# The first loads dealt to two hardware queues, and gate's first weights loaded in halves, in a planned mixture-of-experts kernel

## The chip, the core and the metric

The kernel runs on one core of one Trainium2 chip. The metric is the device time of one execution, in microseconds (us). A profiled execution adds a trace of every engine: PE (TensorE, the matrix engine), ACT (ScalarE), DVE (VectorE), POOL (GpSimd) and SP (SyncE, which here only issues transfers).

## The reference

Nine feed-forward blocks (eight experts and a shared one) are applied to 16 blocks of 256 tokens by 256 features, and their results are mixed with factors of each batch row:

```
g = einsum('bsd,edf->ebsf', h, Wg)          # e = 8, d = 256, f = 1024, float32
u = einsum('bsd,edf->ebsf', h, Wu)
expert_outs = einsum('ebsf,efd->ebsd', silu(g) * u, Wd)
expert_output = einsum('be,ebsd->bsd', gating_probs, expert_outs)
shared = (silu(h @ Sg) * (h @ Su)) @ Sd
x = x + (1 - sg) * expert_output + sg * shared
```

## The kernel before

The work is cut into 72 units: nine sets of weights, two halves of the 1024 hidden features, four groups of four token blocks. Products of several token blocks are not made one by one: the kernel forms sums and differences of inputs and of weights ahead (fast matrix multiplication in the manner of Winograd and Strassen), so TensorE does fewer products and VectorE, GpSimd and ScalarE do more additions. Unit 0 is different. Its weights' sums are not ready yet, so its products are made plainly, one block at a time. These are the "single-block products" of the title, in `unit_up_w` under `if n == 0`.

Nothing is scheduled by hand. Every operation is handed to `Plan.add` with an engine, an assumed length and a rank. `Plan.run` then plays the program through with these lengths: on each engine it takes, of the operations whose inputs are ready and whose buffers are free, the one of the lowest rank. PE alone keeps two strictly ranked lines, one for the products into the `dn` banks and one for all else. The order that comes out is written down engine by engine, and each engine executes its own list strictly in order. So a rank or an assumed length changes the lists, and the lists alone reach the chip. The dictionary `RANK` (lines 25 to 33) holds the constants of these ranks.

What happens at the start matters here. Nine products of zeros (L354) keep PE at work while the first data comes. `make_raw` loads two blocks of x (tile `side`, 256 KB each), transposes each on PE (L561, into `dn`) and copies it with ACT into `pq` (L566). `load_base` loads the upper 128 rows of gate's weights into the first part of a `wb` tile (256 KB) and `load_raw` the lower 128 rows into another `wb` tile (256 KB); up's weights come in the same way. In unit 0 the product of one chunk of 128 hidden features with one token block takes two accumulating matmuls, one with each weights tile. The first two chunks of the first pair of blocks are done one block at a time (moving operand 256 wide, tile X), all later ones for two blocks at once (512 wide, X for gate and M for up).

All these loads go through one helper, whose `engine` argument was left at SP for every load:

```
def load(rank, dst, src, kb, deps=(), new=(), uses=(), late=0, engine="SP"):
    queue = {"SP": nc.sync, "ACT": nc.scalar}[engine]
```

SP's list therefore begins: x block 0, gate's upper rows, gate's lower rows, x block 1, up's upper rows, up's lower rows, x blocks 2 and 3, then gate's and up's other row blocks for the sums, and eight more blocks of x (tiles `h`). PE's list begins, behind the zeros: transposes of block 0; two X products of chunk 0 and one of chunk 1 with block 0; transposes of block 1; the other five X products; two M products; transposes of blocks 2 and 3. A float32 matmul stands in the trace as two records. Two small loads, `p_bc` and `coef` (the mixing factors, spread over all 128 partitions), go out from POOL's queue at the start, and the sums on `wb` and `wp` (L366) begin on POOL once the later weights have landed.

From unit 4 to unit 55 the kernel is in its long middle phase with sums kept in DRAM (tiles `star`); from unit 56 on it uses the other form again and finishes the output.

Of the kernel before, what the change touches and what calls it, by code (L numbers as in the profile page):

```python
# [16 lines left out]
P = 128  # L17
# [5 lines left out]


RANK = {
    "first": 4, "q": 2.85, "dc": 2.45, "acc": 2.55, "g": -5.35, "cp": 1.85, "seed": -0.3, "s": 0.75,
    "lagx": 1.0, "sc": 15.85, "bank": (6.6, 7.1, 8.6, 15.9, 16.4, 16.9, 17.3), "ev": 0.3, "p": 2.3,
    "xc": 0.2, "st": 1.2, "qa": -2.0, "da": -1.25, "ga": -7.25, "pace": 2, "m0": 1.9, "m1": 2.5, "xm":
    0, "w": 16, "mp": 4, "m2": 1.5, "ml": 1.75, "lagw": 1.0, "wp": -0.95, "wq": -0.9, "wqa": -2.25,
    "wdc": 2.2, "ws": 0.5, "wseed": 0.2, "wxc": 0.95, "pa": -4.25, "hd": (), "ph": 7.25, "pd": 1.0,  # L30
    "xh": 5, "hX": 4.5, "hA": 10.5, "hR": 5.0, "hD": -6.5, "hE": 5, "hF": -7.75, "hG": -3.75, "to":
    (-18, -3, -9, -16, -46), "back": (-27, 120, 21, -15, -5, 80, 20),
}


# [169 lines left out]
def kernel(  # L205
# [177 lines left out]
    def load_base(m, e, half, rank, ranks=None):  # L383
        b = Buf("wb", f"wb_{m}_{e}_{half}")
        src = [
            sources(e)[m][ts(part, P), ts(half, 4 * P)].rearrange("p (c q) -> p c q", q=P)
            for part in range(2)
        ] if m < 2 else None
        late = 0 if rank < 0 else 8
        ru, rv = ranks or (rank, rank)  # L390
        if m == 2:
            rows = sources(e)[2][ts(half, 4 * P), :].rearrange("(c p) (k q) -> p c k q", p=P, q=P)
        if m == 2:
            u = v = load(ru, lambda: b.tile, rows, 512, [], [b], late=late)
        else:
            u = load(ru, lambda: b[:, :, 0, :], src[0], 256, [], [b], late=late)
            v = load(rv, lambda: b[:, :, 1, :], src[1], 256, [], [], [b], late=late)
        ops = []
        for i, t in enumerate(POINTS):
            r, x_ = (lambda i=i: b[:, i, 1, :]), (lambda i=i: b[:, i, 0, :])  # L400
            if t == 0:
                op = v
            elif abs(t) == 1:
                op = tt("POOL", rank + 1, r, r, x_, ALU.add if t > 0 else ALU.subtract, P, [u, v], uses=[b])
            elif e == half == 0:
                op = stt(rank + 1, r, x_, float(t), r, ALU.add, P, [u, v], uses=[b])
            else:
                twice = Buf("wp", f"twice_{m}_{e}_{half}")
                op = add(
                    "ACT", act(P), rank + 1, lambda: nc.scalar.mul(twice[:, 0, :], x_(), float(t)), [u, v], [twice], [b]  # L410
                )
                op = tt("POOL", rank + 1, r, r, lambda: twice[:, 0, :], ALU.add, P, [op], [], [b, twice])
            ops.append(op)
        base[m, e, half], baseop[m, e, half] = b, (u, ops)

    def make_pair(m, e, half, k, rank):
        i, j = PAIRS[k]
        d = POINTS[j] - POINTS[i]
        w, (u, rops) = base[m, e, half], baseop[m, e, half]
        b = Buf("wp", f"wp_{m}_{e}_{half}_{k}")  # L420
        r = tt(
            "POOL", rank, lambda: b[:, 0, :], lambda: w[:, j, 1, :], lambda: w[:, i, 1, :], ALU.subtract, P,
            [rops[i], rops[j]], [b], [w],
        )

        def rr():
            return b[:, 0:1, :].broadcast_to([P, 2, P])

        def uu():
            return w[:, i : j + 1 : j - i, 0, :]  # L430

        if d == 1:
            o = tt("POOL", rank, lambda: b[:, 1:3, :], rr, uu, ALU.subtract, 2 * P, [r, u], [], [b, w])
        elif e == 0 and half == 1 and m in RANK["hd"]:
            o = stt(rank, lambda: b[:, 1:3, :], uu, -float(d), rr, ALU.add, 2 * P, [r, u], [], [b, w])
        else:
            o = add(
                "ACT", act(2 * P), rank - RANK["pa"], lambda: nc.scalar.mul(b[:, 1:3, :], uu(), float(d)), [r, u], uses=[b, w]  # L438
            )
            o = tt("POOL", rank, lambda: b[:, 1:3, :], rr, lambda: b[:, 1:3, :], ALU.subtract, 2 * P, [o], [], [b])  # L440
        pair[m, e, half, k], pairop[m, e, half, k] = b, o

    def load_raw(ranks):

        b = Buf("wb", "wb_raw")
        ops = [
            load(
                ranks[m], lambda m=m: b[:, :, m, :],
                sources(0)[m][ts(1, P), 0 : 4 * P].rearrange("p (c q) -> p c q", q=P), 256,
                [], [b] if m == 0 else [], [b] if m else [],  # L450
            )
            for m in range(2)
        ]
        return b, ops

    def load_down(e, half, rank):
# [196 lines left out]
    def diagonal(n, m, unit, a, rank, pq, consume):  # L653

        e, half, g = unit
        w, (u, rops) = base[m, e, half], baseop[m, e, half]
        xb, xo = xd[g, a], xdop[g, a]
        name = f"{m}_{n}_{a}"
        bank = Buf("D", f"D_{name}")
# [3 lines left out]
        for h, i in enumerate((2 * a + 1, 2 * a)):  # L663
            ps.append(
                mm(
                    MM, rank + 1 / 8 + h / 100, lambda h=h: bank[:, h, :], lambda i=i: w[:, i, 0, :],
                    lambda i=i: xb[:, i % 2, :], h == 0, True, h == 1, [u, xo[i][0], *ps],
                    [bank] if h == 0 else [], [w, xb] if h == 0 else [w, xb, bank],
                )
            )  # L670
# [14 lines left out]
        ops = {}  # L685
# [86 lines left out]
    def unit_up_w(n, unit):  # L772
# [41 lines left out]
        if n == 0:  # L814
            w, wops = first_raw
            readers = {0: [], 1: []}
            for step, (a, c) in enumerate((a, c) for a in range(2) for c in range(4)):
                xb, xo = raw[a]
                for m in range(2):
                    b0, (u, _) = base[m, e, half], baseop[m, e, half]  # L820
                    bank = Buf("XM"[m], f"plain_{m}_{a}_{c}")
                    r = 2.6 * step - 7 + m / 2

                    def view(k, xb=xb):
                        return xb.tile[:, 2 * k : 2 * k + 2, :]

                    if m == 0 and step < 2:

                        m1 = None
                        for h in range(2):  # L830
                            rh = -7 + h / 5 + step / 20
                            for k, (wv, wo) in enumerate(
                                ((lambda b0=b0, c=c: b0[:, c, 0, :], u), (lambda c=c: w[:, c, 0, :], wops[0]))
                            ):
                                m1 = mm(
                                    MM, rh + k / 100, lambda bank=bank, h=h: bank[:, h, :], wv,
                                    lambda xb=xb, k=k, h=h: xb.tile[:, 2 * k + h, :], h == k == 0, k == 1, h == 1,
                                    [wo, xo[h], m1], [bank] if h == k == 0 else [],
                                    [w if k else b0, xb] if h == k == 0 else [w if k else b0, xb, bank],
                                )  # L840
                        readers[a].append(m1)
                        gate(f"p{step}")(bank, [m1], r + 0.6, [(c, 2 * a), (c, 2 * a + 1)])
                        continue
                    m0 = mm(
                        2 * MM, r, lambda bank=bank: bank[:, :, :], lambda b0=b0, c=c: b0[:, c, 0, :],
                        lambda view=view: view(0), True, False, False, [u, *xo], [bank], [b0, xb],
                    )
                    m1 = mm(
                        2 * MM, r + 0.1, lambda bank=bank: bank[:, :, :], lambda m=m, c=c: w[:, c, m, :],
                        lambda view=view: view(1), False, True, False, [m0, wops[m], *xo], [], [w, xb, bank],  # L850
                    )
                    readers[a].append(m1)
                    (gate, mult)[m](f"p{step}")(bank, [m1], r + 0.6, [(c, 2 * a), (c, 2 * a + 1)])
# [231 lines left out]
    def unit_down(n, unit, hb, pairs, acc, state):  # L1085
# [3 lines left out]
        for k, (i, j) in enumerate(PAIRS):  # L1089
# [4 lines left out]
            work.append((lambda w=w: w[:, 0, :], wo, lambda gb=gb: gb[:, :], [go], [w, gb]))  # L1094
            work.append((lambda w=w: w[:, 1, :], wo, lambda hbuf=hbuf: hbuf[:, 1, :], lo, [w, hbuf]))
            work.append((lambda w=w: w[:, 2, :], wo, lambda hbuf=hbuf: hbuf[:, 0, :], lo, [w, hbuf]))
        w, (u, rops) = base[2, e, half], baseop[2, e, half]
        for at in range(8):
            i, part = (3 - at, 0) if at < 4 else (at - 4, 1)
            work.append(  # L1100
                (lambda i=i, part=part: w[:, i, part, :], rops[i] if part else u, lambda at=at: acc[:, at, :],
                 state["acc"], [w, acc])
            )
        ev, evops = None, []
# [258 lines left out]
    for n, unit in enumerate(units):  # L1363
# [51 lines left out]
            unit_down(n, unit, *unit_up(n, unit))  # L1415
            continue
        for k in range(NG):
            if n == LAST + min(11 + k, int(RANK["m0"] + RANK["m1"] * k + RANK["m2"])):
                merge(k, W * (LAST + RANK["m0"] + RANK["m1"] * k))
        hb, hops = unit_up_w(n, unit)  # L1420
        if n == end:
# [83 lines left out]
```

## Time and profile before

| | |
|---|---|
| median of 3 runs | 2485.02 us (2485.01 to 2485.07) |
| the profiled execution | 2482.88 us |
| its span, first to last instruction | 2480.8 us |
| PE busy in the span | 2469.3 us |
| DVE, POOL, ACT busy | 1857.2, 1807.2, 1606.0 us |
| bytes moved by DMA | 525.08 MB, mean 212 GB/s |

The span is what the trace shows; the execution's own time is 2.1 us longer, and the unprofiled median lies another 2.1 us higher. PE works through nearly the whole span, so the time can only be shortened where PE stands still or where it would do less.

### The profile page before, as it was taken

How to read it: one execution, taken by the hardware profiler on the slowest of the kernel's cores; microseconds unless marked ns; L12 is line 12 of the kernel's file. 1: busy time of each engine (PE TensorE's matmuls, PEld its weight loads, DVE VectorE, ACT ScalarE, POOL GpSimd, SP SyncE). 2: the span in 40 equal slices, each digit the busy share in tenths (PEclk: the TensorE clock that was granted, in tenths of full speed). 3: DMA queues.
4: the chain of work that ended last, by engine and by line, in shares of the span. 5: the costliest groups of instructions: out<-in, count | busy, mean ns of one | idle time of the engine just before them, and what ended most of it. 6: DMA issues, size and time to landing. Idle time of an engine off the chain costs nothing.

```text
span 2480.8 us, 35084 instructions
## 1 busy us (share of the span) xinstructions
PE 2469.3 (100%) x10894; PEld 2055.7 (83%) x10894; DVE 1857.2 (75%) x3142; ACT 1606.0 (65%) x3373; POOL 1807.2 (73%) x1947
## 2 busy tenths in 40 slices
PE   9999999999999999999999999999999999999999
PEld 5778888888888888888888888888888777777777
DVE  6787777777777777777767777777777788888787
ACT  3357777777787777777777777777777333333331
POOL 6886777768585868677776858586766687877874
PEclk9999999999999999999999999999999999999999
DMA  7545688888898888898888898888888877887666
GB/s 254 184 159 213 211 218 222 209 216 211 222 218 220 207 206 216 213 221 215 216 204 223 210 223 213 208 211 207 220 213 226 235 202 202 217 223 208 172 191 208
DMA packets 195769, 525.08 MB, mean 212 GB/s; under 512 B 16864, under 2 KB 83440, under 8 KB 186112
## 3 DMA queue, kind: packets, MB, share of 16 engines
q0 software_dynamic: 39552, 214.52, 45.1%
q1 hardware_dynamic: 156032, 308.33, 36.2%
q8 instruction: 87, 1.43, 0.2%
q14 instruction: 98, 0.80, 0.1%
HBM read 290.53 MB, written 232.26 MB: 211 GB/s over the span
## 4 chain that ended last, share of the span: by engine, by line
PE 99%; ACT 1%; DMA 0%; DVE 0%; issue 0%; SPq 0%; DVEq 0%
PE dn L647 33%; PE X L647 25%; PE M L647 20%; PE D L647 20%; DMA wb<-in_L_cond_Wg_dram 0%; PE dn L1311 0%; ACT sg L894 0%; PE dn L522 0%; ACT sg L885 0%; PE dn L561 0%; ACT wp L438 0%; SPq L361 0%; DVE X L366 0%; DVEq L1500 0%; ACT pq L674 0%
## 5 line engine op out<-in xcount | busy, mean ns | idle before, releaser
L366 POOL TENSOR_TENSOR s<-pq,pq 128x512 f32<-128x512 f32 x852 | 1116.0, 1337 | 450.0 <-DVE X L366 347.1
L366 DVE TENSOR_TENSOR X<-M,s 128x512 f32<-128x512 f32 x697 | 466.8, 692 | 155.7 <-PE M L647 98.9
L647 PE MATMUL X<-xp,wp 128*128 128x256 f32 x2204 | 570.2, 379 | 0.0
L647 PEld LDWEIGHTS X<-xp,wp 128*128 128x128 f32 x2204 | 418.4, 190 | 82.8 <-issue 24.6
L647 PE MATMUL D<-xd,wb 128*128 128x256 f32 x1760 | 454.6, 380 | 1.4 <-ACT sg L894 0.8
L647 PE MATMUL M<-xp,wp 128*128 128x256 f32 x1732 | 448.3, 379 | 0.3 <-DVE X L366 0.3
L647 PEld LDWEIGHTS D<-xd,wb 128*128 128x128 f32 x1760 | 333.2, 190 | 74.5 <-issue 22.9
L885 ACT ACTIVATE sg<-sg,coef 128x256 f32<-128x256 f32 x832 | 393.1, 510 | 2.4
L647 PEld LDWEIGHTS M<-xp,wp 128*128 128x128 f32 x1732 | 328.8, 190 | 70.6 <-issue 23.2
L1123 ACT COPY ev<-dn 128x512 f32<-128x512 f32 x451 | 261.7, 587 | 137.7 <-PE dn L647 134.7
L366 DVE TENSOR_TENSOR pq<-D,pq 128x256 f32<-128x256 f32 x568 | 229.9, 416 | 107.6 <-PE D L647 101.0
L921 DVE TENSOR_TENSOR big<-big,X 128x1024 f32<-128x1024 f32 x233 | 281.6, 1209 | 0.0
L647 PE MATMUL dn<-h,wp 128*128 128x256 f32 x1040 | 271.6, 379 | 0.5 <-ACT ev L1123 0.4
L366 DVE TENSOR_TENSOR X<-X,sg 128x512 f32<-128x512 f32 x233 | 162.0, 695 | 110.9 <-ACT sg L885 68.9
L674 ACT COPY pq<-D 128x512 f32<-128x512 f32 x284 | 167.2, 589 | 114.4 <-PE D L647 108.0
L647 PEld LDWEIGHTS dn<-h,wp 128*128 128x128 f32 x1040 | 197.2, 190 | 29.4 <-POOL wp L366 0.8
L894 ACT ACTIVATE sg<-X 128x512 f32<-128x512 f32 x236 | 142.0, 602 | 109.0 <-PE X L647 107.4
L647 PE MATMUL dn<-h,low 128*128 128x512 f32 (+1 forms) x498 | 199.0, 503 | 0.0
L1046 ACT COPY ev<-dn 128x512 f32<-128x512 f32 x123 | 72.0, 586 | 163.9 <-PE dn L647 162.7
L1123 ACT COPY big<-dn 128x512 f32<-128x512 f32 x225 | 130.8, 587 | 69.2 <-PE dn L647 67.3
L366 DVE TENSOR_TENSOR low<-X,h 128x256 f32<-128x256 f32 x233 | 97.5, 419 | 94.2 <-ACT h L969 93.8
L647 PE MATMUL M<-xp,low 128*128 128x256 f32 x592 | 157.5, 379 | 0.0
(161 smaller groups left out, 3911.2 us busy)
## 6 DMA issues: line engine op xcount, KB each, us to landing
xp<-keep_p SPq DMA_DIRECT2D x408, 384.0 KB, 5.0
star<-ev POOLq DMA_DIRECT2D x105, 768.0 KB, 6.9
xd<-keep_d SPq DMA_DIRECT2D x136, 512.0 KB, 3.6
star<-big POOLq DMA_DIRECT2D x51, 768.0 KB, 7.0
star<-ev POOLq DMA_DIRECT2D x34, 1024.0 KB, 11.9
total<-ev POOLq DMA_DIRECT2D x18, 1024.0 KB, 7.9
star<-big POOLq DMA_DIRECT2D x18, 1024.0 KB, 11.3
total<-ev POOLq DMA_DIRECT2D x17, 768.0 KB, 6.9
```

What stands on the lines that cost most here:

```text
L366: return add(engine, length, rank, lambda: eng.tensor_tensor(o(), a(), b(), op), deps, new, uses, port=port)
L647: lambda: nc.tensor.matmul(o(), w(), mv(), start=start, stop=stop, skip_group_check=onto),
L674: lambda: nc.scalar.copy(p_[:, 2 - 2 * a : 4 - 2 * a, :], bank[:, :, :]), ps,
L885: lambda: nc.scalar.mul(b[:, h, :], b[:, h, :], coef[:, e, 4 * g + block : 4 * g + block + 1]),
L894: lambda: nc.scalar.activation(b[:, :, :], bank[:, :, :], AF.Silu), deps, [b], [bank],
L921: "DVE", dve(4 * TB), rank, lambda: nc.vector.tensor_tensor(view(), view(), twice(), ALU.add),
L1046: lambda ev=ev, at=at, bank=bank: nc.scalar.copy(ev[:, at, :], bank.tile.rearrange("p a t -> p (a t)")),
L1123: lambda ev=ev, at=at, bank=bank: nc.scalar.copy(ev[:, at, :], bank.tile.rearrange("p a t -> p (a t)")),
```

## The change

The change does four things.

- `load_base` cuts the load of gate's upper rows for unit 0 in two (chunks 0 and 1, then chunks 2 and 3; 128 KB each) and issues both from ACT's queue. `load_raw` does the same with gate's lower rows. Up's loads stay whole and on SP.
- Each product of unit 0 waits for the half that it needs (`us[c]`, `wops[m][c]`) and no longer for the whole tile.
- Sixteen constants of `RANK` have other values; most of them are for the start.
- The bound `11 + k` near the end is written `RANK["w"] - 5 + k`, which is the same number.

```
-            u = load(ru, lambda: b[:, :, 0, :], src[0], 256, [], [b], late=late)
+            parts = 2 if ranks and m == 0 else 1
+            us = [
+                load(
+                    ru + k * 0.4, lambda k=k: b[:, 4 // parts * k : 4 // parts * (k + 1), 0, :],
+                    src[0][:, 4 // parts * k : 4 // parts * (k + 1), :], 256 // parts, [],
+                    [] if k else [b], [b] if k else [], late=late, engine="ACT" if ranks and m == 0 else "SP",
+                )
+                for k in range(parts)
+            ]
+            us = [us[i * parts // 4] for i in range(4)]
...
+        ops = []
+        for m in range(2):
+            parts, src = (2, 1)[m], sources(0)[m][ts(1, P), 0 : 4 * P].rearrange("p (c q) -> p c q", q=P)
+            n = 4 // parts
+            o = [
+                load(
+                    ranks[m] + k * 0.4, lambda m=m, k=k, n=n: b[:, n * k : n * (k + 1), m, :], src[:, n * k : n * (k + 1), :],
+                    256 // parts, [], [b] if m == k == 0 else [], [] if m == k == 0 else [b], engine=("ACT", "SP")[m],
+                )
+                for k in range(parts)
+            ]
+            ops.append([o[i // n] for i in range(4)])
...
-                    b0, (u, _) = base[m, e, half], baseop[m, e, half]
+                    b0, (us, _) = base[m, e, half], baseop[m, e, half]
+                    u, v = us[c], wops[m][c]
...
-                        lambda view=view: view(1), False, True, False, [m0, wops[m], *xo], [], [w, xb, bank],
+                        lambda view=view: view(1), False, True, False, [m0, v, *xo], [], [w, xb, bank],
```

```
 RANK: seed -0.3 -> -0.8, sc 15.85 -> 14.35, p 2.3 -> 2.05, st 1.2 -> 0.95, wq -0.9 -> -0.4,
       wqa -2.25 -> -2.5, pa -4.25 -> -3.5, ph 7.25 -> 7.0, hX 4.5 -> 7.25, hA 10.5 -> 9.75,
       hR 5.0 -> 2.5, hD -6.5 -> -11.25, hE 5 -> 8.5, hF -7.75 -> -8.75, hG -3.75 -> -4.25,
       back (-27, 120, 21, -15, -5, 80, 20) -> (-27, 117, 15, -15, -11, 80, 20)
```

As the lists come out: ACT's begins with the two first halves (upper, lower), then its table load and first activation, then the two second halves. SP's begins with x blocks 0 and 1, up's two loads, x blocks 2 and 3, and goes on as before. PE's has the transposes of block 1 directly behind those of block 0 and then all eight X products of the first two chunks without a break. Further on, the lists of ACT, DVE, POOL, SP and PE differ in order within roughly the first 140 us. Behind that they hold the same instructions in the same order, but for one place of two instructions on DVE, and but for which of several equal tiles (`h` or `big`) a value is put in during the last phase.

## Prediction

> **What bounds the kernel now.** I read the page first, then busy time by stretches, PE's list of waits, PE's and ACT's timeline of the start, and last the time to landing of each early load.
>
> The page says that PE is the bound: 2469.3 of 2480.8 us busy, the chain of waits 99% PE, the granted clock at 9 in all 40 slices.
>
> ```profile
> PE 2469.3 (100%) x10894; PEld 2055.7 (83%) x10894; DVE 1857.2 (75%) x3142; ACT 1606.0 (65%) x3373; POOL 1807.2 (73%) x1947
> PE 99%; ACT 1%; DMA 0%; DVE 0%; issue 0%; SPq 0%; DVEq 0%
> ```
>
> The change takes no product away, so only the 11.5 us in which PE stands still can be gained. The stretches show where they are (columns: stretch, its length, PE busy, then the others, granted clock, DMA share, GB/s):
>
> ```profile
> 0.00:30.00 30.00, 24.92 (x101) 15.13 (x102) 11.51 (x27) 11.03 (x24) 14.97 (x30) 1.00 0.96 288
> 30.00:60.00 30.00, 29.76 (x100) 17.88 (x99) 24.24 (x50) 11.03 (x25) 24.42 (x29) 1.00 0.60 224
> 150.00:300.00 150.00, 149.67 (x661) 124.81 (x660) 111.08 (x182) 109.56 (x235) 111.71 (x132) 1.00 0.60 209
> 1000.00:2000.00 1000.00, 998.34 (x4567) 866.54 (x4566) 732.59 (x1217) 735.07 (x1567) 716.41 (x782) 1.00 0.86 215
> 2460.00:2480.80 20.80, 16.67 (x93) 14.50 (x92) 14.66 (x24) 0.00 (x0) 3.81 (x3) 0.95 0.53 176
> ```
>
> That is 5.08 us at the start, 0.24 and 0.33 soon after, 1.66 in the middle, 4.13 behind the last product (the stores of the output). Of the 5.08, 1.20 lie before the first product of zeros. The other 3.88 are three holes:
>
> ```profile
> 4.61 0.60 PE L561 MATMUL dn<-ident,side 128*128 128x128 f32 x4
> 5.89 0.70 PE L647 MATMUL X<-pq,wb 128*128 128x256 f32 x2 [0.67 <-ACT pq L566]
> 9.55 1.13 PE L647 MATMUL X<-pq,wb 128*128 128x256 f32 x4 [2.97 <-DMA wb<-in_L_cond_Wg_dram]
> 10.52 0.60 PE L561 MATMUL dn<-ident,side 128*128 128x128 f32 x4
> 11.79 1.99 PE L647 MATMUL X<-pq,wb 128*128 128x256 f32 x8 [0.24 <-ACT pq L566]
> 13.62 1.88 PE L647 MATMUL M<-pq,wb 128*128 128x512 f32 x4
> 15.34 0.93 PE L561 MATMUL dn<-ident,side 128*128 128x128 f32 x7
> ```
>
> The reader should see the 2.97 us on gate's lower rows, the third load in SP's list. When the early loads land stands in the transfer view, taken issue by issue (256 KB each, last column: us from issue to landing):
>
> ```profile
> side<-in_x_dram SPq DMA_DIRECT2D x1, 256.0 KB, 2.9
> wb<-in_L_cond_Wg_dram SPq DMA_DIRECT2D x1, 256.0 KB, 3.9
> ...
> wb<-in_L_cond_Wg_dram SPq DMA_DIRECT2D x1, 256.0 KB, 7.8
> side<-in_x_dram SPq DMA_DIRECT2D x1, 256.0 KB, 8.0
> ...
> wb<-in_L_cond_Wu_dram SPq DMA_DIRECT2D x1, 256.0 KB, 8.3
> ```
>
> Issued at 0.75, 1.23, about 1.74, 2.28 and 2.83, they land at 3.7, 5.1, 9.5, 10.3 and 11.1. Up's second load (8.6) lands at 11.9, x blocks 2 and 3 (8.9, 8.5) at about 12.8 and 13.4. Between the second and the third there is a hole in the transfers themselves:
>
> ```profile
> 0.00:5.00 5.00, 3.80 (x13) 1.66 (x13) 0.27 (x1) 1.49 (x2) 1.99 (x8) 1.00 0.50 135
> 5.00:7.00 2.00, 0.91 (x4) 0.30 (x2) 0.00 (x0) 0.59 (x1) 0.00 (x0) 1.00 0.95 96
> 7.00:10.00 3.00, 0.45 (x2) 0.42 (x3) 0.56 (x2) 0.00 (x0) 0.00 (x0) 1.00 1.03 322
> ```
>
> From 5 to 7 us the 16 DMA engines are 0.95 busy and move 96 GB/s; behind it 322. In this spell the two small POOL loads are under way (`p_bc` 5.4 us, `coef` 6.6 us to landing). The change leaves them alone.
>
> **The change part by part.**
>
> *What must land first.* Before, the first X product with both halves of its sum needs x block 0 and both gate loads: 768 KB. After it, PE's list has block 1's transposes second, so nothing goes on before x blocks 0 and 1 and two first halves are there: 256 + 256 + 128 + 128 = 768 KB. The halves save no bytes, since block 1 now comes in their place. They save time in two other ways. Block 1 no longer comes after the 9.55 wait, and the issues go out in parallel: SP's cost 0.43 to 0.51 us each, so three end at 2.24, while two on each of two queues end near 1.75. ACT's own issue time is in no row; I take SP's.
>
> *The landing, bounded from both sides.* A rule of the Trainium skill speaks against the change. "DMA: Bandwidth & Descriptors", section "Issuing engines are not separate DMA queues", says that loads of all queues run on the same 16 DMA engines and mix, so that a second issuing engine saves only the time of issuing. By this rule the 768 KB land at 9.5 - 0.5 = 9.0. The row gives another end. Up to 5.0 us 135 GB/s x 5 = 675 KB have moved; 768 KB are 786 thousand bytes. At the 225 to 271 GB/s of the third and fourth us, half a microsecond more is 112 to 135 KB: 787 to 810 KB by the start of the spell. So the four transfers just about come ahead of it and could land at 5.1 or so, but a landing is that of the slowest of the 16 engines. I take the middle of 5.1 and 9.5, 7.3 us, and keep both ends.
>
> *PE from there.* Block 1's transposes take 4 x 0.109 = 0.43 us, then eight X matmuls (two records of 0.216 each) 3.45 us. ACT's copy of block 1 (0.59) lies beside the first four. M starts at 7.3 + 0.05 + 0.43 + 3.45 = 11.2, against 13.62: 2.4 us earlier. With the rule's 9.0 it is 12.9, 0.7 us earlier. With no wait at all it would be 5.89 + 3.45 = 9.34, but then up's loads decide. They come behind the same bytes as before, so at 11.1 and 11.9 less 0.5; with blocks 2 and 3 at about 12.3 and 12.9 the gain ends at 2.9.
>
> *What is late next.* At 2.4 us the cover is thin. M needs up's second load at 11.2 + 0.86 = 12.1 (lands 11.4), block 2 at 12.95 (12.3), block 3 at 13.4 (12.9), the `h` blocks (5.4 us from issues at 10.3 and 10.9, landing about 15.7 and 16.4 before) at 15.5 and 16.0 (15.2 and 15.9). All just arrive if the stream keeps its 0.5 us.
>
> *ACT's queue.* Four issues stand ahead of ACT's first copy at 5.25. By SP's row they end near 4.2 (two, table load 1.28, activation 0.20, two), so they are hidden under the 3.01 us for which ACT waits before that copy. The other end: SP's seventh and eighth issue took 3.05 us together[...]. If ACT's second pair stalls so until 7, the copy ends at 7.6; with block 1's transposes ending at 7.8 that still costs nothing.
>
> *SP, POOL.* Two issues leave SP, so block 1 and up's loads are issued about 1 us earlier. POOL's list keeps `p_bc` and `coef` first; its sums at 14.26 wait for the later weights and come at most 0.5 us earlier.
>
> *The new ranks.* They reorder ACT, DVE and POOL between about 15 and 140 us. I cost this at zero. PE's holes there (0.24 in 30:60, 0.02 in 100:150) are the most to be gained; on the loss side DVE is nearly full (5.00 of 5 us in 55:60, 19.93 of 20 in 120:140), and if its cover is gone 1 to 2 us come back as waits. Behind 140 us the lists are the same. The 1.66 us in 1000:2000 are waits of 0.2 to 0.5 us each, on ACT (`sg`, `ev`); their sum may move by its whole size either way.
>
> **Sum.** 2482.88 - 2.4 + 0 = 2480.5 for the profiled execution; the median lies 2.14 above it: 2482.6.
>
> **The rivals.**
>
> *Only the issue time is saved.* The spell catches one engine of the 16 and the landing stays at 9.0 to 9.5. Gain 0.2 to 0.7: about 2484.5. For it: the landing of gate's lower rows is the last of 16, and the change does not touch the small loads. Against: the byte count above.
>
> *The clock falls.* The slower side. Before, PE's pause is cut in two by the X product at 5.89, so no hole exceeds 2.97 us and the clock stays 1.00. After, block 1's transposes stand in front of that product, and with a landing at 9.5 PE stands still from 5.04 to 9.5: 4.5 us. The skill's "TensorE: Matmul & The Clock Gate", "What's actually happening", says that after one wholly idle window of about 3.4 us, running freely, the clock is halved until a busy window has passed. The trace agrees as far as it goes: 2.97 us did no harm. A pause of 4.5 holds a whole window in (4.5 - 3.4) / 3.4 = a third of the cases. Price: 3.4 us of products at half pace, 1.7 us, less a gain of 0.2: 2486.5. It decides from a landing later than about 8.5.
>
> *Later waits go too.* The start's gain comes to its cap, the new ranks remove the 0.6 us up to 300 us, and the middle's waits fall away as well: 2.9 + 0.6 + 1.7 = 5.2, so 2479.8.
>
> *New waits behind the start.* DVE or the `h` loads give the gain back and more: 2484 to 2493.
>
> **How the numbers follow.** The likeliest case (landing 5.1 to 8.5) has 0.46, the issue time alone 0.22, later waits gone 0.14, clock 0.07, new waits 0.11. 0.2% of 2485.02 is 5.0 us, about what a measurement of this kernel can tell from no change. Even the full start gain stays inside it; faster by more needs the case in which the later waits go, 0.14; slower by more needs over 7 us of new waits in a stretch of 140 us, or in the last phase by its other tiles, 0.07 of the 0.11; between them 0.79. The range runs from 2479.4 (the 5.2 with a little over) to 2487.0 (clock, or new waits of about 4 us net of the gain).
>
> **What would show it.** Right: in the timeline a single PE hole from 5.04 to about 7.3, released by DMA `side` or `wb`; X x16 without a break; M near 11.2; block 2's transposes near 13; PE busy in 0:30 at about 27.3. Issue time alone: hole to 9 or later, M at 12.9. Clock: a clock under 1.00 in a stretch around 9, X records 0.43 apart. New waits: PE's list of waits has entries of more than 0.5 us between 30 and 140 us, from DVE or POOL. Wrong altogether: a median below 2479 or above 2488.

## The result, and the profile after

| | before | after |
|---|---|---|
| median, same chip | 2484.26 us (2481.35 to 2485.82, 22 runs) | 2480.81 us (2480.59 to 2481.26, 22 runs) |
| profiled execution | 2482.88 us | 2480.82 us |
| its span | 2480.8 us | 2478.8 us |

The ratio of the medians is 0.9988, with a 95% interval of 0.9982 to 0.9993. The changed kernel is 3.45 us faster by the medians and 2.06 us by the two profiled executions. Its runs lie within 0.7 us, those of before within 4.5 us. Both differences will need an explanation.

The stretches of the profile after (stretch, its length, busy time of PE, PEld, DVE, ACT, POOL, granted clock, DMA share, GB/s):

```profile
0.00:5.00 5.00, 3.81 (x9) 1.39 (x10) 0.27 (x1) 1.49 (x2) 1.97 (x8) 1.00 0.66 173
5.00:7.00 2.00, 1.76 (x11) 1.49 (x10) 0.00 (x0) 1.00 (x2) 0.00 (x0) 1.00 0.80 171
7.00:10.00 3.00, 3.00 (x16) 2.64 (x15) 0.17 (x1) 0.54 (x2) 0.00 (x0) 1.00 0.98 258
0.00:30.00 30.00, 27.97 (x110) 17.06 (x111) 14.99 (x34) 12.05 (x27) 18.46 (x33) 1.00 1.00 301
1000.00:2000.00 1000.00, 998.35 (x4567) 866.31 (x4566) 732.51 (x1218) 733.39 (x1565) 715.37 (x781) 1.00 0.87 215
```

Up to 5 us the DMA engines move 173 GB/s where they moved 135, and from 5 to 7 us 171 where they moved 96. PE is busy for 27.97 of the first 30 us (24.92 before). The middle of the kernel is the same to 0.01 us.

The timeline of PE after (start, time, what, and in brackets the idle time ahead of it):

```profile
5.01 1.39 PE L577 MATMUL dn<-ident,side 128*128 128x128 f32 x8
6.64 3.72 PE L663 MATMUL X<-pq,wb 128*128 128x256 f32 x16 [0.24 <-ACT pq L582]
10.20 1.88 PE L663 MATMUL M<-pq,wb 128*128 128x512 f32 x4
11.91 1.04 PE L577 MATMUL dn<-ident,side 128*128 128x128 f32 x8
12.79 1.88 PE L663 MATMUL M<-pq,wb 128*128 128x512 f32 x4
14.50 1.37 PE L538 MATMUL dn<-ident,h 128*128 128x128 f32 x8
...
26.70 0.66 PE L538 MATMUL dn<-ident,h 128*128 128x128 f32 x4 [0.48 <-DVE xd L371]
```

PE no longer waits for gate's weights. The transposes of both blocks run in one go, the X products follow without a break, and M starts at 10.20 instead of 13.62: 3.42 us earlier. Two small holes are new. At 26.70 the third group of `h` transposes in a row needs a `dn` bank that DVE has not read yet, and behind 14.86 a block of `h` is 0.28 us late. Against the 3.42 us at M, the last products of the two traces start only 2.33 us apart (2476.29 and 2473.96). Counted from one start to the next, PE's gaps between 14 and 60 us grew from 0.59 to 1.71 us, which is the 1.1 us that was given back.

Four landings that matter, each taken at its issue:

```profile
side<-in_x_dram SPq DMA_DIRECT2D x1, 256.0 KB, 3.5
wb<-in_L_cond_Wg_dram ACTq DMA_DIRECT2D x1, 128.0 KB, 3.7
...
wb<-in_L_cond_Wu_dram SPq DMA_DIRECT2D x1, 256.0 KB, 6.7
wb<-in_L_cond_Wg_dram ACTq DMA_DIRECT2D x1, 128.0 KB, 6.8
```

The upper two rows are issued at 0.74 and land at about 4.2 and 4.4. The second load of each queue (x block 1, the first half of gate's lower rows) is in by 5.5. The lower two rows are issued at 1.74 and 1.85; they land at 8.4 and 8.7.

### The profile page after: what moved, and what is told of

It reads as the page before. It is cut to its first block, busy times and chain, and to the rows that moved or that the text cites. A ratio compares the mean times of both kernels' runs of the same rounds, so it can differ in the third digit from the quotient of the medians.

```text
span 2478.8 us, 35085 instructions
## 1 busy us (share of the span) xinstructions
PE 2470.1 (100%) x10894; PEld 2056.2 (83%) x10894; DVE 1857.1 (75%) x3142; ACT 1604.6 (65%) x3373; POOL 1806.1 (73%) x1947
## 4 chain that ended last, share of the span: by engine, by line
PE 99%; ACT 1%; DVE 0%; issue 0%; DVEq 0%
PE dn L663 33%; PE X L663 25%; PE M L663 20%; PE D L663 20%; PE dn L1328 0%; ACT sg L911 0%; PE dn L538 0%; PE X L354 0%; ACT sg L902 0%; PE dn L577 0%; ACT wp L450 0%; DVE X L366 0%; DVEq L1517 0%; ACT pq L582 0%; ACT pq L690 0%
## 5 line engine op out<-in xcount | busy, mean ns | idle before, releaser
L663 PE MATMUL dn<-h,low 128*128 128x512 f32 (+1 forms) x486 | 193.7, 501 | 0.0
```

Source lines behind the costliest of these rows:

```text
L663: lambda: nc.tensor.matmul(o(), w(), mv(), start=start, stop=stop, skip_group_check=onto),
```

## The experiments

Theories, as the experiments name them. A: the second queue and the halves bring the first 768 KB in ahead of the spell of the two small POOL loads. B: only one part of this does it (order, halves or queue). C: the new rank constants bring the gain. Later, S, Q, F, P and W are stated with the experiments that test them.

### e1, e2: the new constants taken away, and put in alone

e1 is the changed kernel with the dictionary of before; e2 is the kernel before with the dictionary of after.

```
e1:  RANK = {... "seed": -0.3, "sc": 15.85, "p": 2.3, "hX": 4.5, "hD": -6.5, ...}   # as before, loads as after
e2:  RANK = {... "seed": -0.8, "sc": 14.35, "p": 2.05, "hX": 7.25, "hD": -11.25, ...} # as after, loads as before
```

> The changed kernel with the old constants of RANK: two queues, halves, block 1 second, but the lists behind the start come out otherwise, in the middle phase too. Theory A (the gain is the start: the four first transfers, 768 KB, land before the two small POOL loads take the DMA engines): the first M product starts near 10.2 us as in the changed kernel (10.20; before 13.62), X block without a hole on DMA over 0.5 us; what the run as a whole does is then decided by the middle phase, whose 1.7 us of PE waits may be anything from 0 to some us. Theory C (the constants give the gain): the M product starts after 12 us.

> The kernel before with the new constants of RANK, nothing else. Theory A: first M product at 13.6 us as before, PE hole of about 3 us on gate's lower rows; time within 1 us of before, since the new order of the early lists is made for another start. Theory C: at least 2 us faster than before, ratio 0.9992 or lower.

e1: 2482.67 us (before in the same job 2484.50), ratio 0.9995 (0.9987 to 1.0003). e2: 2484.27 us, ratio 0.9999 (0.9991 to 1.0008). So the constants alone bring no change that can be told from none, and theory C falls. In e1 M starts at 10.27, as theory A expects; still, without the constants half of the start's gain is lost. PE's timeline of e1 shows where, 160 us later:

```profile
170.03 0.59 PE L663 MATMUL dn<-h,wp 128*128 128x256 f32 x2
172.56 0.67 PE L663 MATMUL dn<-low,wp 128*128 128x256 f32 x2 [1.94 <-POOL wp L366]
173.06 3.54 PE L663 MATMUL dn<-h,low 128*128 128x512 f32 x4
176.40 0.67 PE L663 MATMUL dn<-h,wp 128*128 128x256 f32 x2
```

A wait of 1.94 us for POOL, and then four products that take 3.54 us where the same group at 161.47 takes 1.88. The clock explains it. The stretches of e1:

```profile
169.72:173.13 3.41, 1.47 (x8) 0.99 (x7) 2.83 (x6) 1.76 (x4) 3.41 (x5) 1.00 0.79 228
173.14:176.55 3.41, 3.41 (x6) 1.35 (x5) 1.61 (x3) 0.64 (x2) 3.41 (x6) 0.50 0.83 322
```

For 3.41 us the granted clock is 0.50, behind a stretch in which PE worked only 1.47 us. The records of the clock put this spell at 3.413 us; stretches of that length, counted from a change of the clock, are called windows from here on. The runs of e1 show what one costs. A window at half clock lowers a run's mean granted clock by 0.0007. Six runs with a mean of 0.999 (the profiled one among them) took 2483.82 to 2484.58 us, seven with 1.000 took 2482.17 to 2482.67, so about 1.6 us. The median is one of the seven: what it lost, it lost without this window.

e2 shows the same thing in the start, where the loads are those of before (first a stretch, then PE's timeline):

```profile
5.33:8.74 3.41, 1.20 (x7) 0.56 (x5) 0.56 (x2) 0.59 (x1) 0.00 (x0) 1.00 0.99 207
8.68 2.05 PE L647 MATMUL X<-pq,wb 128*128 128x256 f32 x4 [1.54 <-DMA wb<-in_L_cond_Wg_dram]
10.52 1.06 PE L561 MATMUL dn<-ident,side 128*128 128x128 f32 x4
11.37 2.88 PE L647 MATMUL X<-pq,wb 128*128 128x256 f32 x10
14.09 1.88 PE L647 MATMUL M<-pq,wb 128*128 128x512 f32 x4
```

Gate's lower rows came earlier here than in before's first profile (8.68 against 9.55), and still M starts later (14.09 against 13.62): the clock falls at 8.74, and the four X products take 2.05 us instead of 1.13.

### e3, e4: the changed kernel with one queue, and with whole loads

```
e3:  engine="ACT" if ranks and m == 0 else "SP"  ->  engine="SP"     # load_base
     engine=("ACT", "SP")[m]                     ->  engine="SP"     # load_raw
e4:  parts = 2 if ranks and m == 0 else 1        ->  parts = 1       # load_base
     parts, src = (2, 1)[m], ...                 ->  parts, src = 1, ...
```

> The changed kernel with both halves of gate's loads issued from SP: order x block 0, two first halves, x block 1, two second halves, up's loads. The lists behind the start come out otherwise. Theory A (the second queue fills the DMA engines from 2 us on): with one queue the first halves land by about 5, block 1, the fourth transfer, falls in or behind the spell of the small loads and lands at 6 to 9, M at 11 to 13. Theory B (only the order and the halves count, the queue saves no more than its issue time of about 0.5 us a pair): block 1 lands by 6.0, M at 10.2 to 10.8.

> The changed kernel with gate's two first loads whole (256 KB each) on ACT's queue; the second one is issued behind ACT's table load. Behind the start the lists are nearly those of the changed kernel. Now 1024 KB must land before the first sum is complete. Theory A: gate's lower rows land in or behind the spell, 7 to 10 us, M at 11 to 13.5, time 1 to 3 us above the changed kernel. Theory B (the queues alone do it, halves are not needed): M by 10.8, time within 0.6 us of the changed kernel.

e3: 2486.13 us (2483.83 to 2489.12), ratio 1.0010 (1.0001 to 1.0018): slower than before. e4: 2480.22 us (2479.87 to 2482.16, 19 runs), ratio 0.9984 (0.9977 to 0.9991), the lowest median of the study. In e3 x block 1 lands at 8.3 and M starts at 11.48, as theory A expected of one queue. In addition PE works only for 147.06 of the 150 us in 150:300 (149.67 in the changed kernel), so the planner's list for that stretch is a worse one again. This profile is of e3's fastest run; ten of its 13 runs have a mean clock of 0.999 or 0.998, so the median has lost windows too, and it does not tell what the queue alone is worth. PE's timeline of e4:

```profile
4.85 0.60 PE L577 MATMUL dn<-ident,side 128*128 128x128 f32 x4
6.12 0.70 PE L663 MATMUL X<-pq,wb 128*128 128x256 f32 x2 [0.68 <-ACT pq L582]
6.66 0.60 PE L577 MATMUL dn<-ident,side 128*128 128x128 f32 x4
7.10 3.19 PE L663 MATMUL X<-pq,wb 128*128 128x256 f32 x14
10.12 1.88 PE L663 MATMUL M<-pq,wb 128*128 128x512 f32 x4
```

M at 10.12 with whole loads, 10.20 with halves. The halves are not needed. With whole loads the planner also puts block 1's transposes behind the first X product, which lets PE work while ACT copies block 1, and the hole at 26.70 is gone. So the part of Theory A that rests on the halves falls, and of Theory B the form "the queue alone" is left.

### e5, e6, e7: the two small loads out of the way

Theory S: the small loads `p_bc` and `coef` hold up gate's lower rows, and the change helps because it gets past them. Theory Q: one queue cannot bring 768 KB earlier, with or without them.

```
-    nc.gpsimd.dma_start(p_bc...); nc.gpsimd.dma_start(coef[:, E, :], ...)
+    def small(): nc.sync.dma_start(p_bc...); nc.sync.dma_start(coef[:, E, :], ...)
+    small_op = add("SP", 0.5, -16.9, small, lag=2.2)        # behind x blocks 2 and 3
-    coef_op = add("DVE", 0.8, -2, make_coef)
+    coef_op = add("DVE", 0.8, -2, make_coef, [small_op])
```

> The kernel before, with the two small loads (p_bc and coef) issued from SP behind x block 3 instead of from POOL's queue at the start; PE's list is the one of before. Theory S (the small loads hold the 16 DMA engines for some 1.6 us between 5 and 7 us, and gate's lower rows wait behind them): the lower rows land near 7 instead of 9.5, M starts near 11, the median is 1.5 to 2.5 us under before, about 2482. Theory Q (one queue alone does not bring 768 KB earlier, with or without the small loads): the lower rows still land behind 8.5, M starts near 13.5, the median stays within 0.5 us of before.

> The changed kernel with the same move of the two small loads. Theory S: the second halves and up's loads land 1 to 1.5 us earlier, but PE has no DMA wait left at the start that they could shorten, so M stays near 10.2 and the median within 0.4 us of the changed kernel's 2480.8. Theory Q: the same start and the same time. If coef lands behind 12 us, DVE's first products with it are late, and PE waits at the fourth X or M bank: up to 1 us longer.

> The kernel of e4 (gate's two first loads whole, on ACT's queue) with the same move of the two small loads. Both theories: M near 10.1, median within 0.4 us of e4's 2480.2, as the candidate that beats both kernels.

e5, with the loads of before all on SP: 2481.32 us against 2484.11, ratio 0.9990 (0.9981 to 0.9998). e6 (on after): 2480.91. e7 (on e4): 2480.99, where 2480.2 was expected; why it is not as low as e4 is open. So the small loads in their old place cost the kernel before 2.8 us, nearly as much as the whole change brings, and the two remedies do not add up. Theory S holds, Q falls. The start of e5, with the landing of the lower rows above it:

```profile
wb<-in_L_cond_Wg_dram SPq DMA_DIRECT2D x1, 256.0 KB, 4.5
6.74 1.56 PE L651 MATMUL X<-pq,wb 128*128 128x256 f32 x6 [0.68 <-ACT pq L570]
8.14 0.60 PE L565 MATMUL dn<-ident,side 128*128 128x128 f32 x4
8.57 0.60 PE L651 MATMUL X<-pq,wb 128*128 128x256 f32 x2
9.41 1.99 PE L651 MATMUL X<-pq,wb 128*128 128x256 f32 x8 [0.24 <-ACT pq L570]
11.24 1.88 PE L651 MATMUL M<-pq,wb 128*128 128x512 f32 x4
```

PE's order is that of before, but the lower rows are there (landing 4.5 us after the issue at 1.74, so at 6.2 instead of 9.5), and M starts at 11.24. What the small loads do to the DMA engines stands in the transfer view of the first 14 us. Of before (queue, packets, MB, share of the 16 engines' time):

```profile
q1 hardware_dynamic: 4599, 2.97, 71.6%
q0 software_dynamic: 64, 0.07, 11.3%
```

The same view of e5, where POOL's queue has no row:

```profile
q1 hardware_dynamic: 5354, 3.49, 83.4%
```

The packets of POOL's 0.07 MB take 11.3% of 14 us, as much as 1.58 us of each of the 16 engines; those of the other queue's 2.97 MB take 71.6%. In the packet records of before `p_bc` goes as 16 packets of 4096 B of up to 1.2 us, `coef` as 16 packets of 512 B of about 1 us (up to 1.7). Issued from SP, the same `coef` is 128 packets of 64 B that take 8 to 11 ns each.

The trace records each landing in 16 steps, and the last one counts. In before eight steps of gate's lower rows are in by 6.4 us, and the last comes at 9.5; the first step of `p_bc` stands at 4.5, ahead of them all. That a late step comes from an engine with a small packet in front is likely, but the trace does not say which engine a step belongs to.

### e8: one edit on the kernel before

```
-            u = load(ru, lambda: b[:, :, 0, :], src[0], 256, [], [b], late=late)
+            u = load(ru, lambda: b[:, :, 0, :], src[0], 256, [], [b], late=late, engine="ACT" if ranks and m == 0 else "SP")
...
+                [], [b] if m == 0 else [], [b] if m else [], engine=("ACT", "SP")[m],
```

> The kernel before with one edit: gate's two first loads go out whole from ACT's queue; the rank constants are the old ones. Theory A (the second queue makes the start): M near 10.2, with block 1's transposes third in PE's list. If the new constants are needed to keep the lists behind 140 us (Theory C in part), waits of 2 to 3 us return between 150 and 300 us and the median is about 2482.5; if they are not, it is 2480.5.

2480.77 us (2480.41 to 2482.66, 21 runs) against 2484.11, ratio 0.9988 (0.9982 to 0.9995). The landing of gate's lower rows, issued at 1.32, and the start of M:

```profile
wb<-in_L_cond_Wg_dram ACTq DMA_DIRECT2D x1, 256.0 KB, 5.2
9.97 1.88 PE L647 MATMUL M<-pq,wb 128*128 128x512 f32 x4
```

One argument in each of two calls brings what the whole change brings. All 16 steps of the lower rows lie between 6.1 and 6.5, and the first of `p_bc` comes at 6.5. No waits return at 150 to 300 us (PE busy 149.62 of 150), so the new constants are not needed here. In e1 they were missed because halves and old constants together led the planner to another list in that stretch.

### e9: the small loads from ACT's queue instead

Theory F: the form of POOL's packets is what costs. Theory P: their place in time.

```
-    nc.gpsimd.dma_start(p_bc...)          +    nc.scalar.dma_start(p_bc...)
-    nc.gpsimd.dma_start(coef[:, E, :]...) +    nc.scalar.dma_start(coef[:, E, :]...)
```

> The kernel before with one edit: the two small loads go out from ACT's queue instead of POOL's, still at the start, ahead of ACT's table load; all lists but the first places of ACT and POOL are those of before. Theory F (what holds the DMA engines from 5 to 7 us is the form in which POOL's queue sends these loads: 16 packets of 4096 B and 16 of 512 B for about 0.6 and 1 us each): on ACT's queue they cost little, gate's lower rows land near 7, M starts near 11.2 and the median is near e5's 2481.3. Theory P (their place in time, in front of gate's lower rows, is what costs, whatever the queue): lower rows behind 8.5, M near 13.5, median 2484 as before.

2483.60 us against 2484.45, ratio 0.9995 (0.9987 to 1.0003). The profile is of the slowest of its 13 runs (2484.80). The first stretch of e9:

```profile
0.00:5.00 5.00, 3.80 (x9) 1.19 (x9) 0.27 (x1) 1.49 (x2) 0.70 (x6) 1.00 0.24 67
```

and its timeline:

```profile
5.86 1.09 PE L561 MATMUL dn<-ident,side 128*128 128x128 f32 x4 [0.64 <-DMA side<-in_x_dram]
8.03 2.90 PE L647 MATMUL X<-pq,wb 128*128 128x256 f32 x6 [1.07 <-DMA wb<-in_L_cond_Wg_dram]
...
15.04 1.88 PE L647 MATMUL M<-pq,wb 128*128 128x512 f32 x4
```

The long packets are gone, but up to 5 us only 67 GB/s are moved. The small loads now stand ahead of x block 0, which lands at 5.7 instead of 3.7, and of gate's upper rows, at 7.9 instead of 5.1. The lower rows come at 8.8 (7.0 us behind their issue at 1.74). So Theory F falls: the form of the packets alone is not what costs. Theory P has the landing right and the time of M (13.5) wrong, since the pauses also kept PE at half clock until 14.0. The clock column does not show that: it, like the mean clock of a run, counts from the first record of the clock, which stands at 14.02 here, and what lies ahead of it runs at half pace (nine zeros take 4.02 us here; thirteen take 2.97 us in e12, behind the rise). Together with e5: in this kernel these 72 KB are dear wherever they stand in front of what PE waits for, and nearly free behind it. Why so little is moved in the first 5 us of e9 stays open.

### e10, e12: the scatter of the kernel before

Theory W: in many runs of the kernel before, the hole in front of the lower rows lets the clock fall to half for one window. e10 is the kernel before, unchanged. e12 fills the hole with products of zeros, in an unused X bank:

```
+    if step == h == 0 and k == 1:         # ahead of the first product with gate's lower rows
+        for _ in range(13):
+            nc.tensor.matmul(banks[2]..., zero[:, 0:P], zero, start=True, stop=True)   # shortened
```

> The kernel before, unchanged, for a second profile of its start. Theory W (the kernel before sometimes loses one window of half clock in its start, as the profile of e2 showed, and this is why its runs spread over 4 us and their median lies 1.4 us above its first profile): PE's hole before the X products is 2.8 us or more and the granted clock falls below 1.00 somewhere between 7 and 15 us, with a profiled time near 2484 to 2485. If the clock stays at 1.00 and the time is still near 2484, the spread has another cause (a later landing of the lower rows).

> The kernel before with thirteen more products of zeros (0.216 us each at full clock, 2.8 us) behind the first X product, where PE otherwise stands waiting for gate's lower rows; all else is as before. Theory W (in most runs of the kernel before, this hole lets the clock fall to half for one window of 3.41 us, which costs up to 1.7 us on top of the wait): the clock stays at 1.00, M starts at 13.6 to 14 as in the first profile of before, and the median falls from 2484.4 to 2482.5 to 2483.2, with less spread. Rival: the spread comes from the landing of the lower rows alone, or the zeros run into that landing: median 2484 to 2485.

e10, profiled at 2484.18 us (median of 10 runs 2483.91): two stretches, cut at the ends of the clock's windows,

```profile
6.46:9.87 3.41, 0.91 (x3) 0.52 (x4) 0.56 (x2) 0.23 (x1) 0.00 (x0) 1.00 0.96 272
9.88:13.29 3.41, 3.41 (x11) 2.41 (x11) 0.00 (x0) 0.58 (x1) 0.00 (x0) 0.50 1.04 303
```

and M at 15.00 instead of 13.62: the same kernel, with one window of half clock, behind a hole of only 2.21 us (2.8 or more was expected). In before's first profile the windows lie otherwise. Two share the hole, PE works longer in each, and the clock stays up:

```profile
4.19:7.60 3.41, 1.72 (x9) 0.89 (x7) 0.00 (x0) 0.59 (x1) 0.00 (x0) 1.00 0.83 134
7.60:11.01 3.41, 1.46 (x9) 1.31 (x10) 0.56 (x2) 0.00 (x0) 0.00 (x0) 1.00 1.09 335
```

e12: 2483.26 us (2482.67 to 2485.20, 11 runs) against 2484.52. Its profile has the clock at 1.00 throughout and M at 13.95:

```profile
6.47 2.97 PE L845 MATMUL X<-zero 128*128 128x512 bf16 x13
9.88 1.13 PE L647 MATMUL X<-pq,wb 128*128 128x256 f32 x4 [0.44 <-DMA wb<-in_L_cond_Wg_dram]
...
13.95 1.88 PE L647 MATMUL M<-pq,wb 128*128 128x512 f32 x4
```

With work that computes nothing the median is 1.26 us lower, close to what theory W expected (2483.2), and ten of eleven runs lie within 0.7 us. But the interval (ratio 0.9987 to 1.0005) still holds no change. That the clock falls for a window in most runs of before is shown: in the job of e5 to e8, 51 of 65 have a mean granted clock of 0.999, while all 76 runs of e5 to e8 have 1.000, as have all 11 of e12. What this costs before's median is not shown. Its runs with 1.000 have a median of 2483.28 against 2484.11 in that job, but in the job of e1 to e4 the 12 with 1.000 are no faster (2484.53) than the 35 with 0.999 (2484.27). As the mean leaves out a late first rise, a run with 1.000 need not have had an undisturbed start. So the part of theory W about the median stays an estimate.

### e11: fewer products of zeros at the start

```
-    for n in range(9):      # on e4
+    for n in range(7):
```

> The kernel of e4 (gate's two first loads whole, on ACT's queue) with seven instead of nine products of zeros, as x block 0 lands at about 4.3 and the zeros end at 4.6 to 5.0. If the zeros are what is left in front of the transposes: these start 0.3 to 0.5 us earlier and the median is 2479.8 to 2480.0. If the zeros are needed for the clock: it reaches 1.00 one window (3.4 us) later and the median is 1 to 1.7 us above e4's 2480.2.

2481.16 us against e4's 2480.22, with two groups of runs: ten at 2479.55 to 2480.42, ten at 2481.16 to 2481.98, one at 2483.21. The profile is one of the second group:

```profile
4.63 1.08 PE L577 MATMUL dn<-ident,side 128*128 128x128 f32 x4 [0.26 <-DMA side<-in_x_dram]
6.39 1.22 PE L663 MATMUL X<-pq,wb 128*128 128x256 f32 x2 [0.68 <-ACT pq L582]
7.40 1.06 PE L577 MATMUL dn<-ident,side 128*128 128x128 f32 x4
8.26 3.83 PE L663 MATMUL X<-pq,wb 128*128 128x256 f32 x14
11.92 1.88 PE L663 MATMUL M<-pq,wb 128*128 128x512 f32 x4
```

The transposes start 0.22 us earlier than e4's and run at half pace; the clock reaches 1.00 at 9.5 instead of 4.7, and M starts 1.8 us later. In this run the two zeros were missed for the clock, not for the wait. The ten runs of the first group did as well as e4's without them; that their windows lay otherwise fits, but none of them was profiled.

## Why the prediction was right, and where it was not

The forecast was 2482.6, in a range from 2479.4 to 2487.0, most likely within 0.2% of before; it came out at 2480.81, 0.14% below before. The place and the wait were read rightly. That the figure for the profiled execution (2480.5, measured 2480.82) fits so well is luck: M came 1.0 us earlier than forecast, and 1.1 us were given back behind it where nothing was counted. The median was missed by 1.8 us, over half of its change, inside a wide range. Point by point:

- *The place.* Right: all of the gain is in the start, where gate's lower rows were the wait, and the middle's waits did not move (998.34 and 998.35 us busy in 1000:2000).
- *The landing, 7.3 us.* Mis-sized. The four transfers are in by 5.5, near the low end that the byte count gave (5.1). The middle between the two ends was too careful. The Trainium skill's rule ("DMA: Bandwidth & Descriptors", section "Issuing engines are not separate DMA queues"), by which only the issuing time is saved, gave 9.0. The runs do not bear it out here: in e8 the lower rows, as the second load of a queue, are issued 0.4 us earlier (1.32 for 1.74) and land 3.0 us earlier (6.5 for 9.5). What the second queue buys is that the rows no longer wait behind the small loads; e5 shows the same from the other side, with one queue (6.2).
- *M at 11.2, a gain of 2.4.* Mis-sized, for that reason: M came at 10.20, 3.42 earlier, although the clock happened to rise 1.5 us later than in before's profile (5.7 instead of 4.2). The hole from 5.04 to 7.3 that was to show it isn't there; the X products run unbroken, and PE was busy for 27.97 us of 30, not 27.3.
- *The cap of 2.9.* Wrong. It took up's loads to follow the old stream by 0.5 us. They moved up further: 8.4 and 10.4 instead of 11.1 and 11.9. On SP gate's two loads no longer stand ahead of them, so they are issued at 1.74 and 2.25 instead of 2.83 and 3.35.
- *What is late next.* Half right. The `h` blocks cost 0.28 us, as the thin cover let one expect. The 0.5 us wait for DVE in front of the third group of `h` transposes was not seen; it lies in the order of PE's list, which the prediction did not follow so far.
- *ACT's issues hidden.* Right: four issues of about 0.5 us each end before 3.1, the first copy starts at 6.00.
- *The ranks at zero.* Right for the ranks alone (e2) and, with whole loads, for their lack (e8). Not so with the halves: without the new constants e1 is 1.86 us slower than after (in another job). A constant's worth depends on the list it meets.
- *Offset of 2.14 us from the profiled execution to the median.* This term failed for the changed kernel: its median and its profile agree to 0.01 us. It had no reason of its own in the forecast. Before's first profile was one of the runs whose clock did not fall, and most of its runs are not. If e12's 1.26 us is what this costs the median, the change's 3.45 us are, by estimate, about 2.2 to 2.5 us of waiting (2484.26 - 1.26 - 2480.81 = 2.2, or e12's 2483.26 - 2480.81 = 2.45) and the rest the clock; the two profiles, in both of which the clock stayed up, lie 2.06 us apart.
- *The rival "the clock falls".* Its mechanism is real, but on the other side: it strikes the kernel before, and the change takes it away. The clock fell behind windows of 3.41 us in which PE worked for 0.91 us (e10), 1.20 us (e2) and 1.47 us (e1). It stayed behind windows with 1.72 and 1.46 us, the two that share the hole of 2.97 us in before's first profile. So the border lies near 1.5 of 3.41 us; as 1.47 fell and 1.46 stayed, PE's busy time does not place it more finely. Where the windows happen to lie decides what a hole does. The Trainium skill ("TensorE: Matmul & The Clock Gate", "What's actually happening") has the clock halved after an idle window, and the prediction took that as a wholly idle one; in these runs a window less than half busy was enough.

What stays open: why two hardware queues get the lower rows past the small loads so surely. An earlier issue by 0.4 us and a share for each queue at the engines would both do it, and no run here separates them. The landings lean to the first: `p_bc` is issued at 1.31, gate's lower rows at 1.32 in e8, and what is issued at 1.74 lands late there too (up's first load at 8.1 in e8 and 9.5 in e4); but by then 1 MB stands ahead of it. e7 and e8 have four runs of 21 each that lie 1.7 to 1.9 us above their medians; half a window would be 1.7 us, but none of these was profiled. Three of e4's 19 runs and two of e5's 13 lie as far out.

The lowest median is e4's, the change without its halves: 2480.22, against 2480.81 for the changed kernel. They ran in different jobs, each beside the kernel before (ratios 0.9984 and 0.9988 with intervals that overlap), so that e4 beats it is likely and not shown.

## What to carry to other kernels

When the first loads are late, look at what else is in the DMA engines at that moment: here the packets of two small loads of 72 KB in all took as much as 1.6 us of each of the 16 engines, and sending them behind the loads that TensorE waits for brought 2.8 us, nearly as much as a second queue (3.3 in e8). A hole of 1.5 to 2.2 us on TensorE can cost a second time, through the clock (1.6 us in e1); look at the granted clock of the stretch behind it, and profile the kernel more than once when its runs scatter. Where a planner makes the lists, try the smallest edit by itself before new constants are fitted around it.

## What the hardware showed that was not expected

- The clock falls for whole windows of 3.413 us, as the clock records of e1, e2 and e10 show. For the first rise, a window with 2.74 us of PE work was not enough (e11, up to 6.12) and one with 3.02 us was (e10, up to 6.46).
- POOL's queue sends `coef` (8 KB, the same 64 B to every partition) as 16 packets of about 1 us each; SP's and ACT's queues send it as 128 packets of 8 to 11 ns. By e9 the shorter packets alone do not make it cheap in front of other loads.
- ACT issues a DMA in about 0.5 us, like SP, and its table load ran beside the later issues: in after's trace the load starts at 1.78, the third issue at 1.85.
